# A graph-attention kernel: ScalarE writes into a group's gathered places behind the group's last product

## The chip, the cores and the metric

The kernel runs on one core of a Trainium2 chip. The time is device time in microseconds, from the start to the end of one execution. The kernel before was run three times: 2837.4, 2828.61 and 2830.73 us, a median of 2830.73 us.

The engines have short names in the profile: PE is TensorE (matrix products), DVE is VectorE, ACT is ScalarE, POOL is GpSimd, SP is SyncE, which here issues most of the plain transfers. L657 means line 657 of the kernel.

## What is computed

One layer of graph attention over 12500 nodes with 128 features and 200000 edges, in float32. The edges are sorted by their destination.

```
h  = relu(layernorm(x))                                # 12500 x 128
hw = h @ W_node.T          as 4 heads of 32
ew = edge_attr_64 @ W_edge.T
att[e] = a . concat(hw[src[e]], hw[dst[e]], ew[e])     # one number per head
att = leaky_relu(att, 0.2)
m[n]  = max(0, max of att over the edges into n)
ex[e] = exp(att[e] - m[dst[e]])
denom[n] = sum of ex into n + (edges - degree[n]) * exp(-m[n])
out = x + sum over the edges into n of (ex / denom) * hw[src[e]]
```

## The kernel before

**First part.** The node rows are normalised and multiplied by the weights, and a table with 137 numbers per node is written to HBM (128 transformed features, four ones for the sums of the weights, a count, and four source logits). This takes about the first 290 us.

**Tiling of the edges.** 511 edges and one carry entry make a *group* (512 rows, as J = 4 blocks of 128). Four groups make a *quad*. There are 392 groups and 98 quads; mostly four quads make a *super*, over which one softmax is computed. Because the edges are sorted, a group's destinations lie in a window of 96 nodes.

**The gathers.** For each block of 128 edges GpSimd issues one indirect DMA (L140), which fetches the table rows of the edges' sources. They land in `ga`, which has room for eight quads (`QUADS = 8`): quad q + 8 is gathered into the places of quad q. So a gather has to wait until the quad that was there is no longer needed. The last to read a group's places is the multiplication on VectorE that weights the rows (L717). GpSimd has nothing else to do in mid run and issues gathers as early as this allows. A quad's gathered rows are first read when its logits are completed (L541), beside the sums of a quad five places before it.

**One group's sums** (`sums`, L693 to L730). VectorE multiplies the gathered rows with the weights `ex` (L717, into `gw`) and makes the matrix `hot` that says which of 96 window nodes each edge belongs to (L722). ScalarE puts a few columns into `gw` for two groups at a time (L712). TensorE multiplies blocks 1 to 3 (L727) into an accumulator `acc`, of which there are three. Block 0 is left for later, because its first row is the carry: the running sum of the node that was still open at the end of the group before.

**`complete`** is called in each group's step, after L727, and finishes the *group before it*. In order: `complete_group` lets VectorE scale the carry out of row 96 of the accumulator before (L657), which needs that accumulator's last product; TensorE multiplies block 0 (L661), which is the group's last product; `copied` lets ScalarE bring the accumulator of one group further back to SBUF (L666, and per quad L672); `divide` divides and adds x on VectorE for a quad that is ready (L739 to L753), and SyncE writes the result.

**The order of the work** is written out by hand: the generators `sums`, `all_logits` and `softmax` are stepped in turn by `together`, and each engine executes its own instructions in the order in which they are written. So in a group's step TensorE gets L727 of this group, L661 of the group before, and then the logit products of another quad (L524, L527); VectorE gets L717, L722, L657, and then the comparison for those logits (L519). SyncE fetches edge features, destinations and windows (L285, L287, L487, L489). The waits between engines follow from what each instruction reads and writes. Once per super a softmax stands between these steps (L560 to L632), with a chain of scans on VectorE (L576, L601, L603).

Of the kernel before, what the change touches and what calls it, by code (L numbers as in the profile page):

```python
# [26 lines left out]
J = 4  # L27
# [19 lines left out]
def kernel(  # L47
# [35 lines left out]
    nc = tc.nc  # L83
# [365 lines left out]
    with tc.tile_pool(name="work", bufs=2) as work, \  # L449
# [19 lines left out]
        def groups(s):  # L469
            q0, m = supers[s]  # L470
            g0 = quads[q0][0]
            return g0, quads[q0 + m - 1][0] + quads[q0 + m - 1][1] - g0
# [165 lines left out]
        begun, divisions = [], []  # L638
        state = {}

        def complete():


            due = [d for d in divisions if d[0] >= nq - 2 or d[-1] == 1]
            divisions[:] = [d[:-1] + (1,) for d in divisions if d not in due]
            full = state.pop("full", None)
            if begun:
                complete_group(*begun.pop())
            if full:
                copied(*full)  # L650
            for d in due:
                divide(*d[:-1])

        def complete_group(q, i, gw, hot, pt, acc, fc):
            if quads[q][0] + i:
                before = state["before"]
                nc.vector.tensor_tensor(  # L657
                    gw[0:1, 0, 0:H * HW].rearrange("p (h w) -> p h w", w=HW),
                    before[WIN:WIN + 1, 0:H * HW].rearrange("p (h w) -> p h w", w=HW),
                    fc.unsqueeze(2).to_broadcast([1, H, HW]), op=OP.mult)  # L660
            nc.tensor.matmul(acc, hot[:, i, 0, :], gw[:, 0, :], start=False, stop=True)  # L661
            state["before"] = acc
            state["full"] = q, i, pt, acc

# [16 lines left out]
        def marks(q):  # L681

            g0, m = quads[q]
            hot = work.tile([P, QG, J, WIN + 1], F32, name="hot")
            nc.scalar.copy(hot[:, :m, :, WIN], is_last[:, g0:g0 + m, :])  # L685
            if q >= nq - FREE:
                for i in range(m):
                    for j in range(J):
                        nc.gpsimd.tensor_scalar(hot[:, i, j, 0:WIN], lane, slot[:, g0 + i, j:j + 1],  # L689
                                                None, op0=OP.is_equal)  # L690
            return hot

        def sums(q):  # L693

            g0, m = quads[q]
            s = of_quad[q]
            s0, sm = groups(s)
            ga = GA.pop(q)
            heads = lambda t: t[:, :, 0:sm * H].rearrange("p j (h g) -> p j h g", h=H)
            ex, xs, facs = XS[s]  # L700
            fc = facs[WIN:WIN + 1, 0:sm * H].rearrange("p (h g) -> p h g", h=H)
            pt = work.tile([WIN + 1, QG, ROW], F32, name="pt", bufs=3)
            hot = HOT.pop(q) if q in HOT else marks(q)
            for i in range(m):
                g = g0 + i
                if i == 1 and nq > q + 1 >= nq - FREE:
                    HOT[q + 1] = marks(q + 1)

                if i % 2 == 0:
                    gw2 = work.tile([P, 2, J, ROW], F32, name="gw")  # L710
                    n = min(2, m - i)
                    nc.scalar.copy(  # L712
                        gw2[:, 0:n, :, R_CNT:R_SRC + H],
                        xs[:, :, :, g - s0:g - s0 + n].rearrange("p j h g -> p g j h"))
                gw = gw2[:, i % 2]
                by_head = lambda t: t[:, :, 0:H * HW].rearrange("p j (h w) -> p j h w", w=HW)
                nc.vector.tensor_tensor(  # L717
                    by_head(gw), by_head(ga[:, i]),
                    heads(ex)[:, :, :, g - s0].unsqueeze(3).to_broadcast([P, J, H, HW]),
                    op=OP.mult)  # L720
                if q < nq - FREE:
                    nc.vector.tensor_tensor(  # L722
                        hot[:, i, :, 0:WIN], lane_ps.unsqueeze(1).to_broadcast([P, J, WIN]),
                        slot[:, g, :].unsqueeze(2).to_broadcast([P, J, WIN]), op=OP.is_equal)
                acc = ps.tile([P, 512], F32, name="acc", bufs=3)[0:WIN + 1, 0:ROW]
                for j in range(1, J):
                    nc.tensor.matmul(acc, hot[:, i, j, :], gw[:, j, :], start=j == 1, stop=False)  # L727
                complete()
                begun.append((q, i, gw, hot, pt, acc, fc[:, :, g - s0]))
                yield  # L730

        def divide(q, pt, den, lo, hi):
# [84 lines left out]
        with tc.manual_schedule():  # L817
# [8 lines left out]
            for s, (q0, m) in enumerate(supers):  # L826


                ahead = list(range(q0 + m, sum(supers[s + 1]))) if s + 1 < len(supers) else []
                now, ahead = ahead[:1], ahead[1:]  # L830
                beside = [sums(q0 - 1)] if s else late(2) + [raw_scaled(3)]
                if s == len(supers) - 1:

                    for _ in range(2):
                        next(beside[0])
                together(*beside, *map(all_logits, now), softmax(s))
                for k in range(m - 1):
                    now, ahead = ahead[:1], ahead[1:]
                    together(sums(q0 + k), *map(all_logits, now))
                    if s > 4:  # L840
                        next(check_steps, None)
                for a in ahead:
                    together(all_logits(a))
                if not s:
                    complete()
                    complete()
                    together(*late(3))
            flush()
            together(sums(nq - 1))
            for _ in range(3):  # L850
                complete()
# [199 lines left out]
```

## Time and profile before

| what | value |
|---|---|
| median of three runs | 2830.73 us (2828.61 to 2837.4) |
| profiled execution | 2819.46 us, of it the span 2817.6 us |
| VectorE busy | 1370.6 us, 49% of the span |
| TensorE busy (products) | 1413.5 us, 50% |
| GpSimd busy | 1505.0 us, 53% |
| ScalarE busy | 324.5 us, 12% |
| gathers from the table (L140) | 1502, 948 ns each as recorded |
| mean granted TensorE clock | 0.54 of full speed |

A group's line in the profile reads: line, engine, operation, what it writes and reads, the count; then the busy time, the mean of one, and the idle time of its engine just before it, with what ended most of that. In the list of waits the numbers are total microseconds, times, and the longest. In a timeline they are start and duration in microseconds, with the idle time before in brackets. "remote" stands for a release that the profile can't trace to an instruction; "issue" for time in which the engine waited for nothing that shows. The ends of matrix products are modelled, not measured.

### The profile page before, as it was taken

How to read it: one execution, taken by the hardware profiler on the slowest of the kernel's cores; microseconds unless marked ns; L12 is line 12 of the kernel's file. 1: busy time of each engine (PE TensorE's matmuls, PEld its weight loads, DVE VectorE, ACT ScalarE, POOL GpSimd, SP SyncE). 2: the span in 40 equal slices, each digit the busy share in tenths (PEclk: the TensorE clock that was granted, in tenths of full speed). 3: DMA queues.
4: the chain of work that ended last, by engine and by line, in shares of the span. 5: the costliest groups of instructions: out<-in, count | busy, mean ns of one | idle time of the engine just before them, and what ended most of it. 6: DMA issues, size and time to landing. Idle time of an engine off the chain costs nothing.

```text
span 2817.6 us, 26972 instructions
## 1 busy us (share of the span) xinstructions
PE 1413.5 (50%) x7279; PEld 1233.6 (44%) x7279; DVE 1370.6 (49%) x3323; ACT 324.5 (12%) x1187; POOL 1505.0 (53%) x1609
## 2 busy tenths in 40 slices
PE   2433645545445555545545545554544544544475
PEld 1333544434434444444444444444444444443474
DVE  2523444544545554544544554553543544554486
ACT  1532200000000000000000000000000000000011
POOL 7153446556556556556556556556556556555602
PEclk9965555555555555555555555555555555555556
DMA  4242354344343444344344444344344444334330
GB/s 143 98 129 72 93 127 117 95 116 116 96 116 101 118 123 116 100 118 111 104 115 109 102 116 110 98 118 113 95 124 109 103 115 110 103 97 107 96 81 16
DMA packets 214477, 298.95 MB, mean 106 GB/s; under 512 B 86121, under 2 KB 162153, under 8 KB 204914
## 3 DMA queue, kind: packets, MB, share of 16 engines
q1 hardware_dynamic: 162512, 184.97, 24.2%
q0 software_dynamic: 50112, 109.65, 16.2%
q10 hardware_dynamic: 1698, 2.58, 0.3%
q8 instruction: 59, 0.97, 0.1%
q14 instruction: 96, 0.79, 0.1%
HBM read 270.49 MB, written 26.52 MB: 105 GB/s over the span
## 4 chain that ended last, share of the span: by engine, by line
another core or an unknown queue 30%; DVE 28%; PE 11%; issue 9%; POOL 5%; DMA 1%; ACT 1%; SPq 0%; DVEq 0%; POOLq 0%
PE acc L727 5%; DVE at L519 5%; POOL ga L140 5%; DVE gw L717 5%; DVE hot L722 4%; DVE gw L657 3%; PE lg L527 2%; PE acc L661 2%; DVE res L753 2%; DVE res L749 2%; DVE t_ps L601 1%; DVE t_ps L603 1%; DVE U L541 1%; DVE den L744 1%
## 5 line engine op out<-in xcount | busy, mean ns | idle before, releaser
L140 POOL DMA_INDIRECT ga<-table,srci x1502 | 1423.5, 948 | 1165.4 <-DVE gw L717 561.8
L727 PE MATMUL acc<-gw,hot 128*97 128x137 f32 x2352 | 640.4, 443 | 67.2 <-DVE hot L722 21.2
L661 PE MATMUL acc<-gw,hot 128*97 128x137 f32 x784 | 267.5, 444 | 661.5 <-DVE gw L657 578.6
L657 DVE TENSOR_TENSOR gw<-acc,facs 1x132 f32<-1x132 f32 x391 | 115.8, 296 | 922.2 <-remote 823.3
L727 PEld LDWEIGHTS acc<-gw,hot 128*97 128x97 f32 x2352 | 512.5, 276 | 98.5 <-issue 53.0
L661 PEld LDWEIGHTS acc<-gw,hot 128*97 128x97 f32 x784 | 184.8, 274 | 702.5 <-DVE gw L657 610.1
L527 PE MATMUL lg<-wblk,ea 128*128 128x8 f32 x1568 | 404.8, 356 | 0.0
L527 PEld LDWEIGHTS lg<-wblk,ea 128*128 128x128 f32 x1568 | 377.5, 306 | 0.0
L524 PEld LDWEIGHTS <-at 96*128 96x128 bf16 x1568 | 210.3, 164 | 296.4 <-issue 159.8
L666 ACT COPY pt<-acc 97x137 f32<-97x137 f32 x392 | 107.4, 274 | 1870.9 <-DVE gw L657 1517.2
L524 PE MATMUL lg<-pw,at 96*128 96x12 bf16 x1568 | 168.7, 180 | 223.0 <-issue 133.2
L519 DVE TENSOR_TENSOR at<-const_ps,db 96x512 bf16<-96x512 f32 x392 | 267.5, 683 | 14.1 <-DMA db<-in_dst_dram 7.4
L717 DVE TENSOR_TENSOR gw<-ga,ex_ps 128x528 f32<-128x528 f32 x392 | 270.7, 691 | 1.3
L722 DVE TENSOR_TENSOR hot<-const_ps,slot 128x384 f32<-128x384 f32 x384 | 209.9, 547 | 0.0
L619 PE MATMUL ex_ps<-ident,ex 64*128 64x64 f32 (+2 forms) x112 | 18.8, 317 | 202.2 <-ACT ex L608 202.2
L619 PEld LDWEIGHTS ex_ps<-ident,ex 64*128 64x128 f32 (+2 forms) x112 | 14.0, 210 | 205.1 <-ACT ex L608 205.1
L539 DVE TENSOR_REDUCE st<-lg 128x64 f32<-128x192 f32 x98 | 35.1, 358 | 96.9 <-remote 47.2
L386 PE MATMUL row_ps<-wcat,hT 128*128 128x137 f32 x198 | 40.3, 356 | 79.5 <-DVE hT L378 37.2
L689 POOL TENSOR_SCALAR hot<-lane,slot 128x96 f32<-128x96 f32 x32 | 17.1, 555 | 105.2 <-ACT hot L685 94.1
L140 POOL DMA_INDIRECT ga<-in_x_dram,srci x64 | 60.8, 950 | 20.8 <-issue 19.2
L386 PEld LDWEIGHTS row_ps<-wcat,hT 128*128 128x128 f32 x198 | 34.5, 249 | 85.0 <-issue 43.2
L749 DVE TENSOR_TENSOR res<-pt,const_ps 96x512 f32<-96x512 f32 (+2 forms) x102 | 67.5, 662 | 6.1 <-DMA out_dram<-res 1.8
(135 smaller groups left out, 1033.5 us busy)
## 6 DMA issues: line engine op xcount, KB each, us to landing
db<-in_dst_dram SPq DMA_DIRECT2D x98, 768.0 KB
ea<-in_edge_t_dram SPq DMA_DIRECT2D x98, 512.0 KB
ga<-table,srci POOLq DMA_INDIRECT x1502
xw<-in_x_dram SPq DMA_DIRECT2D x392, 48.0 KB
out_dram<-res SPq DMA_DIRECT2D x392, 48.0 KB
pw<-side SPq DMA_DIRECT2D x392, 2.2 KB
table<-row SPq DMA_DIRECT2D x9, 616.5 KB
xt<-in_x_dram SPq DMA_DIRECT2D x9, 576.0 KB
```

The source lines that it names most:

```text
L140: nc.gpsimd.indirect_dma_start(out=ga[:, i, j, 0:width], out_offset=None, in_=rows, in_offset=bass.IndirectOffsetOnAxis(ap=srci[:, g0 + i, ...
L386: nc.tensor.matmul(row_ps[:, t, :ROW], hT[:, t, :], wcat, start=True, stop=True)
L519: nc.vector.tensor_tensor(at[:, i, :], node_ps[0:WIN, g0 + i:g0 + i + 1].to_broadcast([WIN, GE]), db[:, i, :], op=OP.is_equal)
L524: nc.tensor.matmul(lg[:, i, j].rearrange("p k h -> p (k h)"), at[:, i, j * P:(j + 1) * P], sw, start=i + j == 0, stop=False, skip_group_ch ...
L527: nc.tensor.matmul(lg[:, i, 2 * w:2 * w + 2, 0, :], ea[:, i, w, :], wblk, start=False, stop=True, skip_group_check=True)
L657: nc.vector.tensor_tensor(gw[0:1, 0, 0:H * HW].rearrange("p (h w) -> p h w", w=HW), before[WIN:WIN + 1, 0:H * HW].rearrange("p (h w) -> p ...
L661: nc.tensor.matmul(acc, hot[:, i, 0, :], gw[:, 0, :], start=False, stop=True)
L666: nc.scalar.copy(pt[:, i, :], acc)
L717: nc.vector.tensor_tensor(by_head(gw), by_head(ga[:, i]), heads(ex)[:, :, :, g - s0].unsqueeze(3).to_broadcast([P, J, H, HW]), op=OP.mult)
L722: nc.vector.tensor_tensor(hot[:, i, :, 0:WIN], lane_ps.unsqueeze(1).to_broadcast([P, J, WIN]), slot[:, g, :].unsqueeze(2).to_broadcast([P, ...
L727: nc.tensor.matmul(acc, hot[:, i, j, :], gw[:, j, :], start=j == 1, stop=False)
L749: nc.vector.tensor_tensor(res[:, :n, :].rearrange("p g (h d) -> p g h d", d=HD), val[:, :, :, 0:HD], share_ps[:, :n, :].unsqueeze(3).to_br ...
```

## The change

Behind a group's last product (L661) ScalarE copies one number of the accumulator, row 0, column 0, into the first element of each of the group's four gathered blocks, on partition 0. `complete_group` is given `ga` for this. The numbers that were there have been read by then (L717), and the gathers of the quad eight places later overwrite what is written. These gathers now have the copy before them in the same places, and the copy has the group's last product before it.

```diff
-        def complete_group(q, i, gw, hot, pt, acc, fc):
+        def complete_group(q, i, ga, gw, hot, pt, acc, fc):
             if quads[q][0] + i:
                 before = state["before"]
                 nc.vector.tensor_tensor(
...
             nc.tensor.matmul(acc, hot[:, i, 0, :], gw[:, 0, :], start=False, stop=True)
+
+
+            nc.scalar.copy(ga[0:1, i, :, 0:1], acc[0:1, 0:1].unsqueeze(1).to_broadcast([1, J, 1]))
             state["before"] = acc
             state["full"] = q, i, pt, acc
...
                 complete()
-                begun.append((q, i, gw, hot, pt, acc, fc[:, :, g - s0]))
+                begun.append((q, i, ga, gw, hot, pt, acc, fc[:, :, g - s0]))
                 yield
```

## The prediction

> **What bounds the kernel now.** I read the page's table of costly groups first, then the list of waits, then the timeline of a stretch in mid run, GpSimd alone and all engines together. No engine is busy for more than 53% of the span, so waits set the time. The page, its busy times and the two groups that matter:
>
> ```profile
> span 2817.6 us, 26972 instructions
> PE 1413.5 (50%) x7279; PEld 1233.6 (44%) x7279; DVE 1370.6 (49%) x3323; ACT 324.5 (12%) x1187; POOL 1505.0 (53%) x1609
> ...
> L140 POOL DMA_INDIRECT ga<-table,srci x1502 | 1423.5, 948 | 1165.4 <-DVE gw L717 561.8
> ...
> L657 DVE TENSOR_TENSOR gw<-acc,facs 1x132 f32<-1x132 f32 x391 | 115.8, 296 | 922.2 <-remote 823.3
> ```
>
> An instruction of 0.296 us (L657, the carry from group to group) has 823.3 us of idle VectorE time before it, put down to "remote", a release that the profile can't name. The waits, longest first:
>
> ```profile
> ACT pt L666 <- DVE gw L657: 1517.2, 259, 17.8
> DVE gw L657 <- remote: 823.3, 110, 13.9
> PEld acc L661 <- DVE gw L657: 610.1, 85, 12.8
> PE acc L661 <- DVE gw L657: 578.6, 84, 12.5
> POOL ga L140 <- DVE gw L717: 561.8, 94, 9.9
> ```
>
> TensorE and ScalarE wait for L657, and GpSimd's gathers wait for L717, which comes a few instructions behind a late L657 on the same engine. So the question is what L657 waits for. Part of the timeline, all engines (start, duration, engine, line):
>
> ```profile
> 1507.50 0.30 DVE L657 TENSOR_TENSOR gw<-acc,facs 1x132 f32<-1x132 f32 x1
> ...
> 1513.53 0.78 PE L661 MATMUL acc<-gw,hot 128*97 128x137 f32 x2 [1.06 <-DVE gw L657]
> ...
> 1517.03 0.55 DVE L722 TENSOR_TENSOR hot<-const_ps,slot 128x384 f32<-128x384 f32 x1
> ...
> 1517.73 1.66 PE L727 MATMUL acc<-gw,hot 128*97 128x137 f32 x6
> ...
> 1523.37 0.95 POOL L140 DMA_INDIRECT ga<-table,srci  x1 [0.31 <-issue]
> 1527.20 1.82 SPq L489 DMA_DIRECT2D xw<-in_x_dram  x4
> 1527.33 0.30 DVE L657 TENSOR_TENSOR gw<-acc,facs 1x132 f32<-1x132 f32 x1 [9.75 <-remote]
> ...
> 1529.22 0.95 POOL L140 DMA_INDIRECT ga<-table,srci  x1 [4.91 <-DVE gw L717]
> ```
>
> The L657 at 1527.33 reads the accumulator that the product at 1513.53 closed. That product ended, as recorded, at 1514.31; TensorE even ran three later products of the next group at 1517.73. Yet VectorE was let go 13.0 us late, 3.0 us behind the end of the last gather in a run of sixteen (1523.37 + 0.95). The L657 at 1507.50, early in the same run, was not late. The same holds in GpSimd's own timeline:
>
> ```profile
> 1498.20 0.95 POOL L140 DMA_INDIRECT ga<-table,srci  x1 [0.30 <-issue]
> 1504.62 0.95 POOL L140 DMA_INDIRECT ga<-table,srci  x1 [5.47 <-DVE gw L717]
> ...
> 1556.20 0.95 POOL L140 DMA_INDIRECT ga<-table,srci  x1 [7.26 <-DVE gw L717]
> ...
> 1580.70 0.95 POOL L140 DMA_INDIRECT ga<-table,srci  x1 [9.79 <-DVE gw L717]
> ```
>
> So I read it thus: while gathers are issued one behind another, TensorE's word that a product is done arrives late, from about 6 us into a run on, and is given 2.6 to 3.6 us behind the run's end. GpSimd works, then VectorE and TensorE work, by turns. One turn of four quads goes from 1474.44 to 1580.70: 106.3 us with 64 gathers in runs of 20, 16, 16 and 12. The runs take 64 x 1.25 - 4 x 0.3 = 78.8 us, and the four pauses (5.47, 4.91, 7.26, 9.79) 27.4 us. From 420 to 2671 us there are 21.2 such turns.
>
> In words of the Trainium skill: "Perfetto Trace Analysis", section "Tensor Engine Instruction (MATMUL, LD_WEIGHTS)", says that a matmul's recorded end is an estimate and that its update goes out when PSUM has confirmed the write; so the profile alone can't say whether the product or only its word is late.
>
> **The change part by part.** It removes nothing. It adds 392 copies of four elements on ScalarE and three waits.
>
> *The copies.* Nearest rows: ScalarE's 1x16 copy L632 took 198 ns, L672 on 96x16 218 ns, L666 on 97x137 274 ns. I take 0.20 us (bounds 0.15 and 0.27): 392 x 0.20 = 78 us on an engine busy 324.5 of 2817.6 us. Beside other work; without that cover it would be 78 us.
>
> *What is queued behind the copy on ScalarE.* It waits for the group's own last product (L661). Behind it stand L666 of the group before, then L672, L685 and L712. The accumulators have three buffers, so the opening products (L727) of the group after next need that L666, and in every second group L712. So far TensorE could run L727 while the word of L661 was late (1517.73 above); now L727 starts behind the release and L661 of the next group follows it. Price per late release: 1.66 us for L727 and 0.5 for copy and L666, on TensorE. Where L661 isn't late, copy and L666 (0.5 us) lie beside the logit products between (0.22 + 0.57 + 0.20 + 0.57 us): nothing.
>
> *L657 behind the copy.* L666 waits for L657 although both only read one accumulator, so such reads go one by one in program order; the copy, which reads it too, now goes first. That is 0.2 to 0.3 us where L657 is released straight by TensorE. Undisturbed, L657 comes 0.4 us or more after its product and this is hidden. In the last 147 us, without gathers, I count 28 groups x 0.2 = 6 us.
>
> *The gathers' wait.* This decides. The first of each group's four gathers now waits for the copy instead of L717: later by one group's step (about 3 us undisturbed, a late release otherwise). Data come late for nobody: eight quads of places, about three quads (75 us) in hand. But GpSimd can no longer have sixteen gathers free ahead. At a release the copy runs (0.2) and GpSimd starts (0.27 us as from L717's end 1504.35 to 1504.62): 0.5 us after the release, where it now takes 1.90 (1502.72 to 1504.62) or, beside a softmax, 4.25 and 7.20 us. Four gathers take 4.7 us. The next product ends about 3.2 us after the release (L666, L727, L661), early enough in the run not to be late, and frees four more. The third ends about 6.5 us after it, where lateness begins: if it is late, the run ends at eight; if it slips through, at twelve.
>
> The wait behind a run, from the four of this turn: 3.57 us after 20 gathers, 3.01 after 16 (twice), 2.59 after 12; a line through these gives 2.1 after 8 and 1.6 after 4. With 0.5 to restart, a pause is 3.1 us after 12, 2.6 after 8, 2.1 after 4. In the softmax VectorE's scans keep the next group's product away; I take one run of four there with 5.2 us more of pause (7.2 us to the next L717 and 3.2 to its group's product, less the 0.5 + 4.7 us of the four gathers).
> - Runs of twelve: 5 x 3.1 + 2.1 + 5.2 = 22.8 us of pauses in a turn, 4.6 less than now.
> - Runs of eight: 7.5 x 2.6 + 2.1 + 5.2 = 26.8 us, 0.6 less.
>
> I take the middle, since the third product falls on the edge: 2.6 us less per turn, 21.2 x 2.6 = 55 us, less the 6 us at the end: 49 us gained. The profiled execution took 2819.5 us (span 2817.6 and 1.9 around it), so it becomes 2770; the median of the three runs is 11.2 us above it, so the median becomes 2782.
>
> A rule against the change: "SBUF — State Buffer", section "SBUF: two separate sides", says engines and DMA reach the memory through separate ports, so that neither slows the other. By it the gathers wouldn't be why L657 is late, spacing them would win nothing, and only the added waits would stay: the sum would be 2819.5 + 6 and above. The trace speaks the other way (releases 2.6 to 3.6 us behind each run), though none of its rows shows the cause itself.
>
> **The rivals.**
> 1. *Lockstep, slower.* If already the second product after a restart is late, each group's four gathers go alone. For it: GpSimd restarts 1.4 us sooner after a release than now, so whatever had filled up may not have emptied; and SyncE's transfers fall into some runs. Against it: 1507.50, 2.9 us into a run, was on time. All runs of four: 16 x 2.1 + 5.2 = 38.8 us of pauses, 11.4 more per turn, +242 + 6, median 3079. Half fours, half eights: (38.8 + 26.8) / 2 = 32.8, +5.4 per turn, +120, median 2951. It decides from where more than about one run in four ends at four.
> 2. *Lateness all but gone.* If short runs never fill whatever holds the word back, GpSimd's issue bounds: pauses of 8 us per turn, 19.4 less, -411 + 6, median 2426. Against it: TensorE and VectorE free gathers faster (four in about 3 us) than GpSimd issues them (5 us), so runs grow until they hurt.
> 3. *No change.* The waits don't bind, GpSimd being behind anyway: +6 us and less, median 2831 to 2837. Against it: 94 waits of GpSimd for L717.
>
> **How the numbers follow.** A change of 0.3% (8.5 us) is about what a measurement of this kernel can tell from none. The likeliest case, runs of eight to twelve: 0.40, its own range 2730 to 2825, of which 0.03 lies within 0.3%. Rival 1: 0.46. Rival 2: 0.08. Rival 3: 0.06. So faster 0.37 + 0.08 = 0.45, same 0.09, slower 0.46. The predicted time is the likeliest case's, 2782. The range leaves out most of rival 2 and the upper fifth of rival 1: 2620 to 3010.
>
> **What would show it.** Right: runs of eight and twelve gathers in GpSimd's timeline instead of 12 to 20; its waits for ScalarE's copy instead of L717; pauses near 2 to 3 us but more of them; L657's unnamed wait handed to the copy on ScalarE; L727 behind releases. Wrong: runs of four throughout (rival 1); runs as long as now (rival 3); the product's word late with no gather near it, which would take away my reading altogether; or a wait behind short runs as long as behind long ones (3 us after four gathers makes each group 8.2 us instead of 6.6).

## The result and the profile after

The kernel with the change took 2636.14 us (median of four runs, 2618.38 to 2646.86), the kernel before 2829.67 us (median of four, 2814.44 to 2837.4). The ratio is 0.932, with a 95% interval of 0.925 to 0.938: 6.8% faster, 193 us, where 49 us were forecast. As the experiments show further down, this holds on some chips only; on another the change costs 0.3%.

The page of the changed kernel (the copy is L664; behind it lines stand three further down, so L727 is now L730 and L666 is L669):

```profile
span 2644.7 us, 27962 instructions
...
PE 1395.1 (53%) x7279; PEld 1255.2 (47%) x7279; DVE 1371.1 (52%) x3323; ACT 337.7 (13%) x1579; POOL 1508.5 (57%) x1609
...
L140 POOL DMA_INDIRECT ga<-table,srci x1502 | 1427.3, 950 | 1001.0 <-issue 408.5
L730 PE MATMUL acc<-gw,hot 128*97 128x137 f32 x2352 | 645.5, 445 | 500.6 <-ACT pt L669 178.3
...
L657 DVE TENSOR_TENSOR gw<-acc,facs 1x132 f32<-1x132 f32 x391 | 115.9, 297 | 518.2 <-ACT ga L664 425.3
...
L664 ACT COPY ga<-acc 1x4 f32<-1x4 f32 x392 | 60.6, 155 | 1901.7 <-remote 1053.9
```

The engines work as long as before. What shrank is idle time: 1165.4 to 1001.0 us in front of GpSimd's gathers. The unnamed wait ("remote") moved from L657 to the copy, and L657's idle time fell from 922.2 to 518.2 us. The opening products, with 67.2 us of idle time before them until now, have 500.6 us, most of it put down to ScalarE (L669 178.3 us, L715 170.2). The longest waits say the same:

```profile
ACT ga L664 <- remote: 1053.9, 127, 13.7
ACT ga L664 <- PE acc L661: 613.1, 184, 13.3
POOL ga L140 <- issue: 427.7, 1380, 2.0
DVE gw L657 <- ACT ga L664: 425.3, 149, 10.3
POOL ga L140 <- ACT pt L669: 340.8, 104, 7.9
```

TensorE's word still comes late: ScalarE's copy stands for up to 13.7 us behind an unnamed release. GpSimd waits for ScalarE (L669 stands directly behind the copy and hides it in this list), no longer for L717.

GpSimd's own timeline over one turn of four quads, only the gathers that begin a run (start, duration, and in brackets the pause before):

```profile
1482.09 0.94 POOL L140 DMA_INDIRECT ga<-table,srci  x1 [6.79 <-ACT pt L669]
...
1499.57 0.94 POOL L140 DMA_INDIRECT ga<-table,srci  x1 [2.81 <-ACT ga L664]
...
1516.99 0.94 POOL L140 DMA_INDIRECT ga<-table,srci  x1 [2.74 <-ACT pt L669]
...
1534.50 0.94 POOL L140 DMA_INDIRECT ga<-table,srci  x1 [2.84 <-ACT pt L669]
...
1551.99 0.94 POOL L140 DMA_INDIRECT ga<-table,srci  x1 [2.35 <-ACT pt L669]
...
1563.88 0.94 POOL L140 DMA_INDIRECT ga<-table,srci  x1 [2.22 <-ACT pt L669]
...
1577.12 0.95 POOL L140 DMA_INDIRECT ga<-table,srci  x1 [3.56 <-ACT pt L669]
```

From 1482.09 to 1577.12 the turn is 95.0 us long (106.3 before). Its 64 gathers go in runs of 12, 12, 12, 12, 8 and 8, and the six pauses behind them are 16.5 us in all (27.4 before). The pauses are near what the prediction said: 2.35 to 2.84 us behind twelve gathers (3.1 predicted) and 2.22 behind the first eight (2.6). What it did not foresee lies at the softmax, from 1552 on, where it had put a run of four with 7.3 us behind it. All engines there:

```profile
1563.46 0.15 ACT L664 COPY ga<-acc 1x4 f32<-1x4 f32 x1 [6.10 <-PE ex_ps L596]
...
1563.88 0.94 POOL L140 DMA_INDIRECT ga<-table,srci  x1 [2.22 <-ACT pt L669]
...
1566.01 0.15 ACT L664 COPY ga<-acc 1x4 f32<-1x4 f32 x1 [2.23 <-PE acc L661]
...
1566.82 0.14 DVE L599 COPY col<-ex_ps 64x1 f32<-64x1 f32 x1
...
1568.31 1.22 DVE L603 TENSOR_TENSOR_SCAN t_ps<-kp,t_ps 64x511 f32<-64x511 f32 x1
...
1572.70 0.23 DVE L626 COPY facs<-acc 1x64 f32<-1x64 f32 x1 [0.78 <-issue]
```

Two products have freed eight gathers by 1566.01, before VectorE's chain (L599 to L626) begins, and it runs beside these gathers without a wait in front of L599. In the kernel before, the chain of the same softmax came behind a run of twelve, with no gather beside it, since L599 itself stood behind a late word. VectorE's timeline, and a line from the list of waits over the whole trace:

```profile
1573.50 0.15 DVE L599 COPY col<-ex_ps 64x1 f32<-64x1 f32 x1 [6.62 <-remote]
...
1579.46 0.23 DVE L626 COPY facs<-acc 1x64 f32<-1x64 f32 x1 [0.78 <-PE acc L624]
```

```profile
DVE col L599 <- remote: 114.0, 22, 7.0
```

In the changed kernel one such wait of 3.7 us is left. Of the 22 softmaxes between 420 us and the last table gather, L599 starts within a run of gathers in 21; before, it did so in 3.

Summed over the trace from 420 us to the last table gather, I split the pauses of GpSimd (over 0.6 us) into those that touch a softmax, from 3 us before its first scan (L576) to 10 us behind the start of L601, and all others.

| | before | after |
|---|---|---|
| beside a softmax: pauses, us | 42, 330 | 58, 209 |
| elsewhere: pauses, us | 52, 227 | 76, 196 |
| together, us | 557 | 405 |

So there are more pauses, and they are 152 us shorter in all: 121 us beside the softmax and 31 elsewhere. How this splits depends on where "beside" ends: with 5 us behind L601 in place of 10, as in the expectation of e18 below, the column after reads 115 and 290, because the pause behind the gathers that run beside the chain then counts as elsewhere; the column before stays as it is. A further 12 us came off at the end, where nothing is gathered any more (145.6 to 133.3 us behind the last gather). The two spans differ by 172.9 us (2817.6 and 2644.7); the 9 us that remain lie in the same stretch, between these pauses, and weren't traced further.

### The profile page after: what moved, and what is told of

It reads as the page before. It is cut to its first block, busy times and chain, and to the rows that moved or that the text cites. A ratio compares the mean times of both kernels' runs of the same rounds, so it can differ in the third digit from the quotient of the medians.

```text
span 2644.7 us, 27962 instructions
## 1 busy us (share of the span) xinstructions
PE 1395.1 (53%) x7279; PEld 1255.2 (47%) x7279; DVE 1371.1 (52%) x3323; ACT 337.7 (13%) x1579; POOL 1508.5 (57%) x1609
## 5 line engine op out<-in xcount | busy, mean ns | idle before, releaser
L140 POOL DMA_INDIRECT ga<-table,srci x1502 | 1427.3, 950 | 1001.0 <-issue 408.5
L730 PE MATMUL acc<-gw,hot 128*97 128x137 f32 x2352 | 645.5, 445 | 500.6 <-ACT pt L669 178.3
L730 PEld LDWEIGHTS acc<-gw,hot 128*97 128x97 f32 x2352 | 509.3, 275 | 541.9 <-ACT pt L669 184.6
L657 DVE TENSOR_TENSOR gw<-acc,facs 1x132 f32<-1x132 f32 x391 | 115.9, 297 | 518.2 <-ACT ga L664 425.3
L524 PEld LDWEIGHTS <-at 96*128 96x128 bf16 x1568 | 220.1, 167 | 311.8 <-issue 137.8
L664 ACT COPY ga<-acc 1x4 f32<-1x4 f32 x392 | 60.6, 155 | 1901.7 <-remote 1053.9
L524 PE MATMUL lg<-pw,at 96*128 96x12 bf16 x1568 | 170.2, 181 | 249.3 <-issue 110.8
L661 PE MATMUL acc<-gw,hot 128*97 128x137 f32 x784 | 255.9, 429 | 0.6 <-DVE gw L657 0.6
L661 PEld LDWEIGHTS acc<-gw,hot 128*97 128x97 f32 x784 | 198.2, 282 | 0.9 <-DVE gw L657 0.9
L569 PE MATMUL t_ps<-ident,U 128*64 128x128 f32 (+2 forms) x112 | 28.7, 409 | 184.7 <-DVE U L565 151.1
L569 PEld LDWEIGHTS t_ps<-ident,U 128*64 128x64 f32 (+2 forms) x112 | 14.0, 149 | 189.7 <-DVE U L565 153.6
L669 ACT COPY pt<-acc 97x137 f32<-97x137 f32 x392 | 100.9, 258 | 0.0
L140 POOL DMA_INDIRECT ga<-in_x_dram,srci x64 | 60.6, 947 | 20.9 <-issue 19.2
```

Of the source, the lines that this page charges most:

```text
L140: nc.gpsimd.indirect_dma_start(out=ga[:, i, j, 0:width], out_offset=None, in_=rows, in_offset=bass.IndirectOffsetOnAxis(ap=srci[:, g0 + i, ...
L524: nc.tensor.matmul(lg[:, i, j].rearrange("p k h -> p (k h)"), at[:, i, j * P:(j + 1) * P], sw, start=i + j == 0, stop=False, skip_group_ch ...
L657: nc.vector.tensor_tensor(gw[0:1, 0, 0:H * HW].rearrange("p (h w) -> p h w", w=HW), before[WIN:WIN + 1, 0:H * HW].rearrange("p (h w) -> p ...
L669: nc.scalar.copy(pt[:, i, :], acc)
```

## The experiments

Theory 1: the gathers' wait for the copy wins, since it shortens the runs and lets GpSimd start again at the release. Rival A: the new order of the reads of the accumulator wins. Within theory 1, theory 1a says that the gain lies at the softmax, and rival B that short runs win the same wherever they are.

### On the first chip no word is late

The first four kernels ran on a chip where the kernel before takes **2034.47 us**, not 2830.

**e1: the copy writes elsewhere.**

```diff
+    aside = consts.tile([1, QG, J], F32, name="aside")
...
-            nc.scalar.copy(ga[0:1, i, :, 0:1], acc[0:1, 0:1].unsqueeze(1).to_broadcast([1, J, 1]))
+            nc.scalar.copy(aside[0:1, i, :].unsqueeze(2), acc[0:1, 0:1].unsqueeze(1).to_broadcast([1, J, 1]))
```

> The copy on ScalarE stays behind the last product and still reads the accumulator, but writes into a place of its own; the gathers wait for the multiplication (L717) as in the kernel before. Theory 1 (the gain comes from the gathers' wait for the copy): none of the 193 us is left; 2830 us plus at most 40 for the opening products that now start behind the release: 2825 to 2870 us, runs of 12 to 20 gathers as before. Rival A (the gain comes from the order in which ScalarE and VectorE read the accumulator): as the changed kernel, 2620 to 2655 us.

2039.56 us, 1.0026 of before (1.0016 to 1.0036). Neither theory had foreseen the level. The page of e1 on this chip (L140 is L141, L657 is L658):

```profile
span 2038.3 us, 27214 instructions
...
L141 POOL DMA_INDIRECT ga<-table,srci x1502 | 1429.2, 952 | 472.6 <-issue 384.5
...
L658 DVE TENSOR_TENSOR gw<-acc,facs 1x132 f32<-1x132 f32 x391 | 115.9, 296 | 88.8 <-ACT aside L665 79.0
```

A gather costs GpSimd the same (952 ns and 0.3 us behind it), but all 1502 go in one run of 1886.8 us without a pause, and L657 has 88.8 us of idle time before it, none of it unnamed. There is no late word here, and GpSimd's issue sets the time. This is what the prediction's second rival described, except that nothing in the kernel brought it about: it came with the chip.

**e2: VectorE writes instead of ScalarE.**

```diff
+                gone, k = state["places"]
+                nc.vector.tensor_copy(gone[0:1, k, :, 0:1],
+                                      before[0:1, 0:1].unsqueeze(1).to_broadcast([1, J, 1]))
...
-            nc.scalar.copy(ga[0:1, i, :, 0:1], acc[0:1, 0:1].unsqueeze(1).to_broadcast([1, J, 1]))
             state["before"] = acc
+            state["places"] = ga, i
```

> The write into the gathered places is made by VectorE, directly behind the carry's multiplication (L657) of the next group, which reads the same accumulator; ScalarE has no new instruction. Theory 1: the gathers are released by the same product, some 0.4 us later (L657 0.30 us and the write 0.1), while the opening products (L727) no longer queue behind the release (1.66 us earlier on TensorE): of the 193 us at least three quarters stay, 2580 to 2690 us, with runs of 8 to 16. Rival A (it is ScalarE's order that matters): 2800 to 2870 us.

2580.98 us, 1.268 of before: much slower, and for a reason of my own making. One group later is too late for a quad's last group: by then the gathers of the quad eight places on stand in the program already, so VectorE's write waits for those new gathers to land, and overwrites one number in each of four of their rows. The list of waits shows it (the write is L662):

```profile
DVE ga L662 <- DMA ga<-table,srci: 910.3, 79, 13.5
```

79 waits, for 98 quads. It tells nothing of the theories, but it shows what the place is worth: the same write one group later turned a transfer that had slack into the bound.

**e3, e4: copies in half of the quads.** The edit of e3; e4 has `not in` in place of `in`.

```diff
+            q0, m = supers[of_quad[q]]
+            if q in (q0, q0 + m - 1):
-            nc.scalar.copy(ga[0:1, i, :, 0:1], acc[0:1, 0:1].unsqueeze(1).to_broadcast([1, J, 1]))
+                nc.scalar.copy(ga[0:1, i, :, 0:1], acc[0:1, 0:1].unsqueeze(1).to_broadcast([1, J, 1]))
```

> The copies are made only for the first and the last quad of each super, beside which the softmax lies, half of all copies. In the turn looked at, the pauses around the softmax fell from 7.26 + 9.79 to 2.35 + 2.22 + 3.56 us (28 gathers each), the others from 5.47 + 4.91 to 2.81 + 2.74 + 2.84 (36 gathers each): 8.9 against 2.0 us. Theory 1a (the gain lies in the softmax, whose scans now have a run of gathers beside them): 8.9 / 10.9 of 193 = 158 us are left, 2670 us (2640 to 2710). Rival B (short runs win the same everywhere): half, 2733 us (2715 to 2760).

> The copies are made only for the quads in the middle of each super, the other half. Theory 1a (the gain lies in the softmax): 2.0 / 10.9 of 193 = 35 us are left, 2795 us (2770 to 2825). Rival B (short runs win the same everywhere): half, 2733 us (2710 to 2755). If gathers of the quads without copies just run ahead and take over, nothing: 2830 us.

2038.63 and 2035.96 us, 1.0024 and 1.0012 of before. Without late words there is nothing to win.

### The change again, on a second chip

> The changed kernel itself once more, beside the kernel before. On the chip of the first four runs the kernel before took 2034 us where it had taken 2830, and its gathers went in one run of 1502 without a pause. Theory 1b (the change wins only where TensorE's word comes late during gathers; this is a state of a chip): where the kernel before takes about 2034 us, the changed kernel takes the same within 0.5%, 2030 to 2045 us; where the kernel before takes about 2830, the changed one about 2640. Rival C (the change wins 6.8% everywhere): 1895 us beside 2034.

> The kernel whose copies write to a place of their own, once more. Where the kernel before takes about 2830 us: theory 1 says 2825 to 2870, rival A (the order of the reads of the accumulator) 2620 to 2655. Where it takes about 2034 us: 2040 again, and it tells nothing apart.

The kernel before took 2033.51 us here, the changed one **2038.63, 1.0030 of it (1.0017 to 1.0043): slower by 0.3%**. e6 took 2037.79 (1.0019). Rival C falls: the gain of 6.8% is not had everywhere, and it was met only where words are late.

**e7: no gathers from the ninth quad on** (the kernel before with wrong rows there).

```diff
-            for j in range(n):
+            for j in range(n if q < QUADS or rows is x else 0):
```

> The kernel before without its gathers from the ninth quad on: it computes with the rows of the first eight quads in place of the others. Where the kernel before takes about 2830 us: if the gathers are why the word is late, every late release goes and four quads take about 70 us as in the last 147 us, 1900 to 2050 us in all; if something else makes it late, at least 2400 us. Where the kernel before takes about 2034 us, with GpSimd issuing without a pause: 290 us at the start and 98 quads at 15 to 17.5 us, 1760 to 2000 us; it shows how much slack the others have behind GpSimd.

1694.2 us (one run) beside 2033.51. So on such a chip the gathers set the time, 339 us above what the other work needs. For late words it tells nothing, there being none.

### A chip with late words: which part of a gather holds them back

On the third chip the kernel before took **2988.72 us**.

**e8: plain transfers in place of the gathers.**

```diff
+                if q >= QUADS:
+                    r0 = ((g0 + i) * J + j) % (NP // P) * P
+                    nc.gpsimd.dma_start(ga[:, i, j, 0:width], rows[r0:r0 + P, :])
+                    continue
                 nc.gpsimd.indirect_dma_start(
```

> The kernel before, in which GpSimd fetches 128 rows of the table that lie side by side with a plain transfer in place of each gather from the ninth quad on; so it computes with wrong rows there, but the bytes, the places, the queue and the waits are the same. Where the kernel before takes about 2830 us: if it is GpSimd's making of a gather's list of addresses that holds the word of TensorE back, the late releases go, 2050 us or less; if it is the transfers and their completions, they stay, 2500 to 2850 us. Where the kernel before takes about 2034 us: if the plain transfer costs GpSimd as much to issue (0.95 + 0.30 us), 2034 again; if it costs less, down to the 1694 us of the kernel without gathers.

1966.1 us, a third less, one run each, with the same bytes, packets and queue. The page (the plain transfers are L142, L657 is L661):

```profile
span 1964.0 us, 26972 instructions
...
L142 POOL DMA_DIRECT2D ga<-table x1438 | 762.4, 537 | 811.2 <-DVE gw L721 569.9
...
L661 DVE TENSOR_TENSOR gw<-acc,facs 1x132 f32<-1x132 f32 x391 | 115.8, 296 | 62.1 <-PE acc L665 53.8
```

L657's wait is 62.1 us in all, 53.8 of it released by the product itself. The transfers are not what holds the word back.

**e9: the copy writes elsewhere, on this chip** (the kernel of e1).

> The kernel whose copies write to a place of their own. Where the kernel before takes about 2830 us: theory 1 (the gathers' wait for the copy wins) says 2825 to 2870, rival A (the order of the reads of the accumulator wins) 2620 to 2655. Where it takes about 2034 us: 2038 again.

3013.75 us beside 2988.72, one run each, so 1.008 of before and no gain. Rival A falls: with the same copies, in the same order, and without the gathers' wait, nothing is won. Its list of waits (L727 is L731, L717 is L721):

```profile
ACT aside L665 <- remote: 1410.3, 131, 17.3
DVE gw L658 <- ACT aside L665: 958.5, 170, 13.8
POOL ga L141 <- DVE gw L721: 746.3, 88, 13.4
PEld acc L731 <- ACT pt L670: 740.7, 84, 12.3
PE acc L731 <- ACT pt L670: 732.5, 85, 12.2
```

The copies bring their costs here (the opening products stand 732.5 us behind ScalarE), and the runs stay at 16 gathers with pauses of mostly 7 to 13 us.

**e11: a list of indices again, but of rows that lie side by side.** On a fourth chip, where the kernel before took 2970.45 us.

```diff
+    rows_on = consts.tile([P, 16], I32, name="rows_on")
+    nc.gpsimd.iota(rows_on, pattern=[[P, 16]], base=0, channel_multiplier=1)
...
+                k = ((g0 + i) * J + j) % 16
+                at = rows_on[:, k:k + 1] if q >= QUADS else srci[:, g0 + i, j:j + 1]
...
-                    in_offset=bass.IndirectOffsetOnAxis(ap=srci[:, g0 + i, j:j + 1], axis=0))
+                    in_offset=bass.IndirectOffsetOnAxis(ap=at, axis=0))
```

> The kernel before, whose gathers from the ninth quad on fetch 128 rows that lie side by side, still by a list of indices, in place of the edges' sources; so it computes with wrong rows there. With the plain transfers of the same rows the late releases were gone. Where the kernel before takes 2800 to 3000 us: if it is the issue by a list of indices that holds TensorE's word back, it takes the same as the kernel before (within 3%), with runs of 12 to 20 gathers; if it is the scattered reads of the table, GpSimd runs without a pause and it takes about 2034 us. Where the kernel before takes 2034: 2034 in both cases.

2968.44 us, 0.9999 of before (0.9965 to 1.0032). The waits (L657 is L661, L140 is L144):

```profile
DVE gw L661 <- remote: 1002.4, 128, 14.2
...
POOL ga L144 <- DVE gw L721: 687.4, 89, 13.3
```

All late words are back, so scattered rows aren't the reason: between e8 and e11 only the form of the instruction differs in kind, a plain transfer (537 ns of GpSimd) or one by a list of indices (954 ns). Where a chip has late words, it is the issue by a list that holds them back; whether by the list itself or by the longer time that each takes on GpSimd, these two runs don't separate.

### The changed kernel and a later copy, on the fourth chip

> The changed kernel a third time, to stand beside the other kernels of this call and the kernel before on the same chip. Where the kernel before takes 2800 to 3000 us: 5 to 9% less than it, as in the comparison (ratio 0.932); where it takes 2034: 2039 as on the second chip.

2660.33 us from two runs, 0.900 of before (0.877 to 0.924): the gain is there again, and larger.

**e12: the copy stands behind L669.**

```diff
             if full:
                 copied(*full)
+            if "write" in state:
+                to, k, of = state.pop("write")
+                nc.scalar.copy(to[0:1, k, :, 0:1], of[0:1, 0:1].unsqueeze(1).to_broadcast([1, J, 1]))
...
-            nc.scalar.copy(ga[0:1, i, :, 0:1], acc[0:1, 0:1].unsqueeze(1).to_broadcast([1, J, 1]))
             state["before"] = acc
+            state["write"] = ga, i, acc
```

> As the changed kernel, but the copy stands on ScalarE behind the copy of the accumulator of the group before (L669 in the changed kernel), no longer ahead of it. So the opening products of the next group but one (L730) no longer queue behind a late release by way of L669, only in every second group by way of L715. Where the kernel before takes 2800 to 3000 us: theory 1 says 20 to 60 us less than the changed kernel, since up to 1.66 us of products lie ahead of the release in half of some 140 releases; if L730's place behind the release costs nothing (the products find time beside the gathers), the same within 10 us. Where it takes 2034: 2035 to 2040.

2640.58 us (2637.04 and 2644.12), 19.8 us less than e10 (2655.78 and 2664.89), at the lower edge of what was expected. That is two runs each, which don't overlap, on a chip where runs of the kernel before lay up to 49 us apart, so the size is uncertain. By way of L669 the opening products no longer wait; by way of L715 they do (the copy is L653 here, L730 is L733, L715 is L718):

```profile
ACT ga L653 <- remote: 1025.0, 143, 11.7
...
PEld acc L733 <- ACT gw L718: 335.2, 82, 9.5
PE acc L733 <- ACT gw L718: 320.8, 79, 9.1
```

This version is the fastest of those that ran on that chip. On a chip without late words it wasn't tried.

### Pacing, and where the gain lies

**e13, e14, e16: GpSimd fills a small tile behind each gather,** twice, and eight times in e14.

```diff
+    idle = consts.tile([P, 40], F32, name="idle")
...
                     in_offset=bass.IndirectOffsetOnAxis(ap=srci[:, g0 + i, j:j + 1], axis=0))
+                for _ in range(2):
+                    nc.gpsimd.memset(idle, 0.0)
```

> The kernel before, in which GpSimd fills a small tile twice (128x40, used by nothing) behind each gather, so that gathers come at some 1.35 to 1.5 us instead of 1.25. In the kernel before the word of TensorE came 2.59, 3.01 and 3.57 us behind runs of 12, 16 and 20 gathers, and 10.1 us behind a run of 64 at the start: 0.6 + 0.15 us per gather. Theory 2 (a gather needs about 1.40 us of something that GpSimd loads every 1.25 us, and TensorE's word waits until this is empty): from a distance of 1.40 us on nothing piles up, the word comes in time, and GpSimd goes without pauses: 1566 x 1.45 + 160 = 2430 us (2300 to 2550), where the kernel before takes 2800 to 3000. Rival D (gathers hold the word back whatever their distance): the pauses stay and 1566 x 0.2 us come on top, 3100 to 3300 us. Where the kernel before takes 2034: 2300 to 2500, no word being late there.

> The same with eight fills behind each gather, a distance of some 1.6 to 1.9 us. Theory 2: no late word, 1566 x 1.75 + 160 = 2900 us (2650 to 3150), slower than with two fills, VectorE's unnamed waits at L657's place below 100 us in all. Rival D: 3400 us and more. The true distance is read from the trace, and by theory 2 the time is 1566 times it and some 160 us.

> The kernel with two fills behind each gather, once more. On a chip where the kernel before took 2034 us it took 2515, with gathers 1.43 to 1.85 us apart (mean 1.5). Where the kernel before takes 2800 to 3000 us: theory 2 (a backlog of 0.15 us per gather at a distance of 1.25 us, none from 1.40 us on) says 2515 us here too (2480 to 2600), that is faster than the kernel before by some 15%, with no late word and no pauses; rival D (gathers hold the word back whatever their distance) says 3100 to 3400 us.

All three fell on chips without late words (before 2034.0 and 2033.38 us): 2514.63, 4268.91 and 2508.93 us. There a fill is simply GpSimd's time; two of them bring gathers from the table to a distance of 1.43 us and more, 1.57 on the mean (e13), eight to 2.56 and more. Theory 2 (a backlog of 0.15 us per gather) wasn't tested and stays open.

**e15, e17, e18: the kernel of e3 until it met late words.**

> The copies only for the first and last quad of each super, as in e3, now beside late words if the chip has them. Where the kernel before takes about 2970 us and the changed one 2660: theory 1a (the gain lies in the softmax, 8.9 of 10.9 us per turn by the pauses of the turn looked at) says 0.82 of the gain, about 2715 us (2690 to 2770); rival B (short runs win the same everywhere) half of it, 2815 us (2780 to 2860). In proportion where the kernel before takes less; where it takes 2034, 2038 again.

> The copies only for the first and last quad of each super. Where the kernel before takes about 2970 us and the changed one 2660: theory 1a (the gain lies in the softmax) says 0.82 of the gain, about 2715 us (2690 to 2770); rival B (short runs win the same everywhere) half of it, 2815 us (2780 to 2860). Where it takes 2034, 2038 again.

> The copies only for the first and last quad of each super. Summed over the 22 softmaxes between 420 us and the last gather, GpSimd's pauses beside a softmax (from 3 us before its first scan to 5 us behind the first of the two scans over the edges that end it) fell from 330 to 115 us in the comparison, and all other pauses rose from 227 to 290 us; on another such chip, from 283 to 102 and from 397 to 314 us. Theory 1a (the gain lies in the softmax): where the kernel before takes 2800 to 3000 us, at least 0.7 of the changed kernel's gain of 190 to 310 us is left, 2620 to 2750 us. Rival B (short runs win the same everywhere): half, 2735 to 2830 us. Where the kernel before takes 2034: 2038 again, and it tells nothing apart.

e15 and e17 met none (2037.45 and 2039.13 us, 1.0021 and 1.0031 of before). e18 ran on the chip of e10: **2885.28 us, 0.971 of before (0.966 to 0.976)**, 91 us of gain beside the 310 of e10. That is three tenths, less than theory 1a (seven tenths and more) and less than rival B (half). GpSimd's timeline, the gathers that begin a run in one turn:

```profile
1523.22 0.94 POOL L140 DMA_INDIRECT ga<-table,srci  x1 [2.95 <-ACT ga L666]
...
1561.36 0.94 POOL L140 DMA_INDIRECT ga<-table,srci  x1 [8.48 <-DVE gw L722]
...
1596.80 0.94 POOL L140 DMA_INDIRECT ga<-table,srci  x1 [15.79 <-ACT pt L671]
...
1608.73 0.94 POOL L140 DMA_INDIRECT ga<-table,srci  x1 [2.26 <-ACT pt L671]
...
1615.40 0.94 POOL L140 DMA_INDIRECT ga<-table,srci  x1 [1.98 <-ACT pt L671]
...
1633.04 0.94 POOL L140 DMA_INDIRECT ga<-table,srci  x1 [2.96 <-ACT ga L666]
```

Gathers into the quads without copies run ahead, 24 and then 16 at a stretch, up to 1581 us. The word that they hold back comes at 1584.24, and only then does the work begin that leads to the first product with a copy, beside the softmax: a pause of 15.79 us. From 420 us on, the 18 pauses behind runs of sixteen are 15.5 us each, 279 of 659 us in all. At the softmax itself the copies do what they do in the changed kernel: L599 has no unnamed wait, and the 22 runs of eight have 2.3 us of pause behind them. So both numbers fall, but the experiment doesn't tell where the full change gains, since the quads without copies made runs of up to 28 gathers, where the kernel before has at most 20 from 420 us on. What it shows is that short runs at the softmax are worth little when the runs ahead of it stay long.

## Why the prediction was wrong

The direction of the sum and most of the mechanism held; the size did not. That it went this way was no better than even by the prediction's own chances (0.45 for faster, 0.46 for slower). Step by step:

- **What bounds the kernel.** The reading was right for the chip that it was made on, and for two others. It left out that this is no property of the kernel alone: on four chips no word is late. Nothing in one chip's trace could show that.
- **The copies.** 0.155 us each, 60.6 us in all, not 0.20 and 78; hidden.
- **What is queued behind the copy.** Right in kind: L730 waits for L669 and L715. e12 prices the part by way of L669 at some 20 us for the whole kernel, from two runs.
- **L657 behind the copy.** 6 us were added for the stage without gathers; it became 12 us shorter instead. Less work is left there: 450 of TensorE's product records behind the last gather instead of 482, where a group has 16.
- **The gathers' wait, runs and pauses.** Right: from 420 us on mostly runs of twelve and eight, pauses with medians of 2.8 and 2.4 us where 3.1 and 2.6 were worked out, and GpSimd held by ScalarE in place of L717.
- **The softmax: the step that failed.** "In the softmax VectorE's scans keep the next group's product away; I take one run of four there with 5.2 us more of pause (7.2 us to the next L717 and 3.2 to its group's product, less the 0.5 + 4.7 us of the four gathers)." No such extra is there. From 420 us on, the changed kernel's 134 pauses stand behind 85 runs of twelve gathers, 28 of eight, 17 of four and 4 of sixteen. With the prediction's own pauses for these (3.1, 2.6, 2.1 and, by its line, 3.5 us) and no extra they would be 386 us; they measure 405. That leaves 19 us for 22 softmaxes, 0.9 us each, not 5.2: of the 110 us that 21.2 turns put into the sum, some 90 are too much. In e10 the same reckoning gives 408 us, and 417 are measured. The 7.2 us in that step were the way from a late L599 to the next L717, with no gather beside it; in the changed kernel L599 is not late, and in 21 of 22 softmaxes its chain begins beside a run of eight or twelve gathers, where four had been counted. Why L596's word comes in time now is argued from the turn shown, where the copy at 1563.46 is put down to that very product; no run tests it alone.
- **Eight or twelve.** The middle between the two cost another 30 us: 21.2 turns at 19.6 us are 416 without the softmax, beside the 386 above, since the runs were mostly of twelve. Together with the softmax that is 121 of the 123 us by which the prediction's profile (2770) lies above the measured one (2646.9).
- **The turn that stood for all.** It had 27.4 us of pauses, 581 us in 21.2 turns; the whole trace has 557, so 24 us less could be won. The stretch without gathers (18 us better than said) and the 9 us that weren't traced make up for that.

Of the rivals, the first (lockstep) can be seen in 21 of 144 runs of table gathers that are four long, fewer than the one in four from which it would have decided. The third, the added waits alone (+6 us), gives about the number met on a chip without late words, 2033.51 to 2038.63 us; on the same chip the copies into a place of their own (e6, +4.3 us) cost nearly as much.

The rule of the Trainium skill that was weighed, in "SBUF — State Buffer", section "SBUF: two separate sides" (engine and DMA traffic can't slow each other), would have had the sum end at +6 us. On two kinds of chip both are seen. Where no word is late, +5.1 us agrees with it. Where words are late, e11 against e8 shows an engine's word held back by GpSimd's issue of gathers, and there the measurement decides against that sum; the rule speaks of ports to the memory, and no run here shows that a port is what is contended.

## What to carry to other kernels

Where one engine's long waits are put down to no instruction, and they end a fixed time behind another engine's bursts, look at how long the bursts are: tying the burst to the consumer's progress, for every group, can win several per cent. But measure on more than one chip before building on it, since here the same change wins 7 and 10% on two and loses 0.3% on a third. And when a pause is estimated from an engine that is kept away, ask whether it will still be kept away at that place, and count what will be under way beside it: here four gathers were counted, and eight or twelve ran.

## What the runs showed of the hardware

- **Two kinds of chip.** Six chips were met behind the prediction. The kernel before took 2033.4 to 2034.5 us on four and 2970 to 2989 us on two; the comparison's own was 2830. The granted clock of the kernel before (0.52 to 0.54 as a mean) and the time of a gather on GpSimd (0.95 us) are the same on both kinds. One of the two with late words was met twice, with two of the others in between, and was the same both times; for the rest a state that passes can't be told from a property of the chip.
- **On the one kind, gathers by a list of indices hold back TensorE's word, and more than that.** The trace records when a semaphore changes. Each of the eight that count landed gathers is raised 16 times for each of 195 or 196 gathers, 3120 or 3136 times. In e1 the trace shows 3015 to 3096 separate changes of each; in the kernel before, on the other kind of chip, 363 to 567. The same kernel as e1 on such a chip (e9): 349 to 540, and with plain transfers there (e8), 2890 to 2925. The eight semaphores of SyncE's plain transfers, 2832 to 2880 rises each, show the same: 1283 to 1337 changes in the kernel before, 2696 to 2775 in e1, 2768 to 2806 in e8. So the rises of the semaphores arrive in bunches, on this kind of chip and while gathers go by a list, and not those of the gathers alone. What part of the chip does this stays open.
- **The delay at the start.** Where words are late, the table comes later too: the first gather from it starts at 164.2 us in the kernel before and at 98.0 us in e1 on the first chip. In e8, whose 64 gathers at the start still go by a list, it is 164.7 us. That these 64 are the reason fits, but wasn't tested alone.
